# Projections by seven block products: queries, keys and values of a masked attention layer on one core

## The chip, the cores and the metric

One Trainium2 chip, one of its cores. The time is the device time of one launch in microseconds (us), the median of several runs. Engines of the core: TensorE (PE in the profile; PEld is its loading of stationary operands), VectorE (DVE), ScalarE (ACT), GpSimd (POOL) and SyncE (SP), which here only issues DMAs. Each engine runs its own queue of instructions in order; queues wait for each other by semaphores.

## The reference

32 graphs of 512 nodes with 512 features share one adjacency matrix. Layer 0 is a masked attention of 8 heads of 64 features, layer 1 a graph convolution; each is added to its input and normalised over the features. All is float32.

```
q, k, v = x @ Wq + bq, x @ Wk + bk, x @ Wv + bv      # each 512x512 by 512x512, per graph
scores = q k^T / 8 + (0 where adj else -1e9)         # per head
out = softmax(scores) @ v
x = layernorm(x + out)
y = adj @ x                                          # per graph
x = layernorm(x + y @ weight + bias)
```

## The kernel before

One fast path does the work (a general path follows only if a check at the end asks for it; here it does not run). Its order is written out by hand in program order; the tile framework adds only the waits. All matrices are held as four blocks of 128 rows, on 128 partitions.

**Projections.** `x_transpose(b, c)` (L264) turns one block of graph b's rows by TensorE and ScalarE copies it into `xT`. `project_qk(b, hp, which)` (L272) makes one block of 128 features of the queries or keys, transposed: four matmuls of 128x128 stationary and 512 moving columns into one bank of PSUM. ScalarE takes the bank for queries (L281), VectorE for keys (L283). `project_v` (L285) does the same for one block of rows of the values, taken by VectorE (L292). That makes 12 units per graph. PSUM banks for everything but scores and attention outputs come from a ring of three, `bank` (L205): the n-th user waits until the (n-3)-th has been read.

**Attention.** The main loop runs over pairs (graph b, pair of heads hp). In each step it issues `scores` for the next pair of heads in two halves (matmuls L379, exponential on ScalarE L382, mask product on VectorE L383, running sum on GpSimd L386 and L388), with `attend` (L396) for the present pair between them. Every second step also adds up the denominators (L407), inverts them (`invert`, L420 to L423) and adds the attention output of two pairs to the rows (`residual`, L429 to L434).

**Work in between.** The end of each step takes units from a list that is made new for each graph (at hp = 0). It holds, in order: the 12 projection units of graph b+1; among them `normalise` of graph b-1 (both layer norms due: ScalarE takes a root, L317, VectorE a reciprocal and eight blocks of rows, L321), `split` of graph b-1 (rows into a rounded part `high` and a rest `low`, one operation of 128x2048 each, L327 and L328) and `store` of graph b-2; then `aggregate` (adj @ x, eight matmuls on the high and low parts, L350, in fp32r) alternating with the transposes of graph b+2; then `convolve` (y @ weight, L360, the sum on VectorE L362, after GpSimd has added the bias row, L355). Each unit has a weight (1.0, 0.6, 0.15 or 0), and `work_until` spreads the weights evenly over the four steps:

```
begin = share * (hp - begun) + (0.25 if hp % 2 else 0.0)
end = share * (hp - begun + 1) + (0.0 if hp % 2 else 0.25)
while units and (units[0][1] == 0 or done < begin + (end - begin) * part - 0.3):
```

**Loads.** The rows of a graph are loaded once, into one of four buffers `xs`, which is transposed, added to, normalised and at last stored. All DMAs go through SP's queue, in program order. At the start the three projection weights are loaded whole, in rows of 2 KB.

Of the kernel before, what the change touches and what calls it, by code (L numbers as in the profile page):

```python
# [27 lines left out]
FP = mybir.dt.float32  # L31
# [8 lines left out]
NEG = -1.0e9  # L40
P = 128
HD = 64
GROUP = 4
BOUND = 1.0e20


def load_row(nc, pool, v, name):
    t = pool.tile([P, v.shape[0]], FP, name=name)
    nc.sync.dma_start(t, bass.AP(tensor=v.tensor, offset=v.offset, ap=[[0, P], [1, v.shape[0]]]))
    return t  # L50


def load_col(nc, pool, v, name):
    t = pool.tile([P, v.shape[0] // P], FP, name=name)
    nc.sync.dma_start(t, v.rearrange("(c p) -> p c", p=P))
    return t


def load_weight(pool, w, name, queue):
    t = pool.tile([P, w.shape[0] // P, w.shape[1]], FP, name=name)  # L60
    queue.dma_start(t, w.rearrange("(c p) f -> p c f", p=P))
    return t
# [127 lines left out]
def fast_kernel(ctx: ExitStack, tc, verdict, x, adj, Wq, bq, Wk, bk, Wv, bv, W1, b1, out):  # L190
# [14 lines left out]
    def bank(*shape):  # L205

        return psum.tile([P, *shape], FP, name="bank", tag="bank", bufs=3)


    X = {}  # L210

    def load(b, by_block=False):
        X[b] = work.tile([P, NB, D], FP, name="xs", bufs=4)
        if by_block:
            for c in range(NB):
                nc.sync.dma_start(X[b][:, c, :], x[b, c * P:(c + 1) * P, :])
        else:
            nc.sync.dma_start(X[b], x[b].rearrange("(c p) d -> p c d", p=P))

    load(0, by_block=True)  # L220
    wq = load_weight(consts, Wq, "wq", nc.sync)
    wk = load_weight(consts, Wk, "wk", nc.sync)
    bq_c = load_col(nc, consts, bq, "bq_c")
    bk_c = load_col(nc, consts, bk, "bk_c")
    adj_s = work.tile([P, NB, N], FP, name="yT", bufs=1)
    nc.sync.dma_start(adj_s, adj.rearrange("(c p) m -> p c m", p=P))
    wv = load_weight(consts, Wv, "wv", nc.sync)
    bv_r = load_row(nc, consts, bv, "bv_r")
    for b in range(1, min(3, B)):
        load(b)  # L230
    w1 = load_weight(consts, W1, "w1", nc.sync)
    b1_r = load_row(nc, consts, b1, "b1_r")

    ident = consts.tile([P, P], FP, name="ident")
    make_identity(nc, ident)
# [25 lines left out]

    XT, QT, KT, V = {}, {}, {}, {}

    def x_transpose(b, c):  # L264
        if c == 0:
            XT[b] = work.tile([P, DB, N], FP, name="xT", bufs=1)
        pt = bank(DB, P)
        for d in range(DB):
            nc.tensor.transpose(pt[:, d, :], X[b][:, c, d * P:(d + 1) * P], ident)
        nc.scalar.activation(XT[b][:, :, c * P:(c + 1) * P], pt, AF.Copy)  # L270

    def project_qk(b, hp, which):  # L272
        w, bias, store, name = (wq, bq_c, QT, "qT") if which == 0 else (wk, bk_c, KT, "kT")
        if hp == 0:
            store[b] = work.tile([P, HP, N], FP, name=name)
        pm = bank(N)
        for d in range(DB):
            nc.tensor.matmul(pm, w[:, d, hp * P:(hp + 1) * P], XT[b][:, d, :],  # L278
                             start=(d == 0), stop=(d == DB - 1))
        if which == 0:  # L280
            nc.scalar.activation(store[b][:, hp, :], pm, AF.Identity, bias=bias[:, hp:hp + 1])  # L281
        else:
            nc.vector.tensor_scalar(store[b][:, hp, :], pm, bias[:, hp:hp + 1], None, op0=ALU.add)  # L283

    def project_v(b, c):  # L285
        if c == 0:
            V[b] = work.tile([P, NB, D], FP, name="v")
        pm = bank(D)
        for d in range(DB):
            nc.tensor.matmul(pm, XT[b][:, d, c * P:(c + 1) * P], wv[:, d, :],  # L290
                             start=(d == 0), stop=(d == DB - 1))
        nc.vector.tensor_add(V[b][:, c, :], pm, bv_r)  # L292

    def flips(b):
        return [(x_transpose, b, c) for c in range(NB)] if b < B else []

    def projections(b):
        if b >= B:
            return []
        units = [(project_qk, b, hp, w) for hp in range(HP) for w in range(2)]  # L300
        return units + [(project_v, b, c) for c in range(NB)]

# [16 lines left out]
            nc.vector.tensor_scalar(row, row, STAT[t][:, slot, 0:1], rstd[:, slot:slot + 1],  # L321
                                    op0=ALU.subtract, op1=ALU.mult)

    def split(b):
        high = HIGH[b] = work.tile([P, NB, D], FR, name="high", bufs=1)
        low = LOW[b] = work.tile([P, NB, D], FR, name="low", bufs=1)
        nc.scalar.activation(high, X[b], AF.Copy)  # L327
        nc.vector.tensor_sub(low, X[b], high.bitcast(FP))  # L328

    def norms(t):  # L330

        parts = [(normalise, t, range(2 * NB if t > 0 else NB)), (split, t)]
        return parts + [(store, t - 1)] * (t > 0) if t >= 0 else []

    def store(b, blocks=None):
        for c in blocks or ():
            nc.sync.dma_start(out[b, c * P:(c + 1) * P, :], X[b][:, c, :])
        if blocks is None:
            nc.sync.dma_start(out[b].rearrange("(c p) d -> p c d", p=P), X[b])


    YT = {}

    def aggregate(b, d):
        if d == 0:
            YT[b] = work.tile([P, DB, N], FP, name="yT", bufs=1)
        pm = bank(N)
        for part in (LOW[b], HIGH[b]):
            for m in range(NB):
                nc.tensor.matmul(pm, part[:, m, d * P:(d + 1) * P], adjT[:, m, :],  # L350
                                 start=(part is LOW[b] and m == 0), stop=(part is HIGH[b] and m == NB - 1))
        nc.scalar.activation(YT[b][:, d, :], pm, AF.Copy)  # L352
        if d == DB - 1:
            for c in range(NB):
                nc.gpsimd.tensor_add(X[b][:, c, :], X[b][:, c, :], b1_r)  # L355
# [7 lines left out]
        statistics(b, 1, c)  # L363

    def aggregation(b):
        return [(aggregate, b, d) for d in range(DB)] if b >= 0 else []

    def convolution(b):
        return [(convolve, b, c) for c in range(NB)] if b >= 0 else []
# [4 lines left out]
    def scores(b, hp, half):  # L374
        for j in (2 * half, 2 * half + 1):
            ps = psum.tile([P, 2, N], FP, name="ps", bufs=2)
            for s in range(2):
                lanes = slice(s * HD, (s + 1) * HD)
                nc.tensor.matmul(ps[:, s, :], KT[b][lanes, hp, j * P:(j + 1) * P], QT[b][lanes, hp, :],  # L379
                                 start=True, stop=True)  # L380
            e = E[b, hp, j] = work.tile([P, 2, N], FP, name="e", bufs=6)
            nc.scalar.activation(e, ps, AF.Exp, scale=1.0 / root)  # L382
            nc.vector.tensor_mul(e, e, edge[:, j, None, :].to_broadcast([P, 2, N]))  # L383
            if j == 1:
                ES[b, hp] = work.tile([P, 2, N], FP, name="es", bufs=3)
                nc.gpsimd.tensor_add(ES[b, hp], E[b, hp, 0], e)  # L386
            elif j > 1:
                nc.gpsimd.tensor_add(ES[b, hp], ES[b, hp], e)  # L388

    def attend(b, hp):  # L390
        po = psum.tile([P, N], FP, name="po", bufs=1)
        for j in range(NB):
            e = E.pop((b, hp, j))
            for s in range(2):
                h = 2 * hp + s
                nc.tensor.matmul(po[s * HD:(s + 1) * HD, :], V[b][:, j, h * HD:(h + 1) * HD], e[:, s, :],  # L396
                                 start=(j == 0), stop=(j == NB - 1))
        AT[b, hp] = work.tile([P, N], FP, name="attT")
        nc.scalar.activation(AT[b, hp], po, AF.Copy)
# [55 lines left out]
    def run(units):  # L455
        for unit in units:
            unit[0](*unit[1:])

    first = projections(0)
    run(flips(0) + first[:4])  # L460
    for c in range(NB):
        adjacency(c)
        run(first[4 + 2 * c:6 + 2 * c])

    pairs = [(b, hp) for b in range(B) for hp in range(HP)]
    scores(*pairs[0], 0)
# [2 lines left out]
    for i, (b, hp) in enumerate(pairs):  # L469
        if hp == 0:  # L470


            units = [(u, 1.0) for u in projections(b + 1)]
            for k, chore in enumerate(norms(b - 1)):
                units.insert(2 * k + 1, (chore, 0.0))
            gather, turn = aggregation(b - 1), flips(b + 2)
            for k in range(NB):
                units += [(u, 0.6) for u in gather[k:k + 1]] + [(u, 0.15) for u in turn[k:k + 1]]
            if b < B - 1:
                units += [(u, 1.0) for u in convolution(b - 1)]  # L480

            begun = 0 if b < B - 1 else 1
            share = sum(w for _, w in units) / (HP - 2 * begun)
            done = 0.0
        if hp == 1 and b > 0 and b + 2 < B:
            load(b + 2)

        def work_until(part):

# [26 lines left out]
            run([u for u, _ in units])  # L516
    run([u for u, _ in units])
    t = B - 1
    rest = convolution(t - 1)
    run(rest[:2])  # L520
    invert(t, 1)
    residual(t, 2)
    residual(t, 3)
    normalise(t, range(NB))
    split(t)
    run(rest[2:])
    if t > 0:
        normalise(t, range(NB, 2 * NB))
        store(t - 1)
    run(aggregation(t))  # L530
    judge()
    for c in range(NB):
        convolve(t, c)
# [26 lines left out]
```

## Time and profile before

| | before |
|---|---|
| median of 3 runs | 3242.62 us (3241.83 to 3243.03) |
| the profiled execution | 3243.45 us, span 3241.7 us |
| its mean granted TensorE clock | 0.997 |
| VectorE, ScalarE, GpSimd busy | 1498.2, 995.7, 1183.0 us |
| matmuls of the projections, busy | wq 466.8, wk 463.5, wv 456.4 us |
| matmuls of scores, attention, convolution, busy | 510.7, 467.7, 458.2 us |
| rows of normalise (L321), mean of one | 646 ns |
| DMA moved | 74.73 MB, mean 23 GB/s |

The profile is of one execution. A line of its list of groups gives the source line, engine and operation, the output and inputs with partitions and elements, the number of instructions, the busy time in us and the mean duration of one in ns, then the engine's idle time just before them and what ended it. Matmuls are pipelined, so that the mean duration of one is longer than the distance from one to the next. A line of the timeline has a start and a duration in us, and merges neighbours of one kind; in brackets stand the idle time before it and what ended that.

### The profile page before, as it was taken

What the parts mean: (1) busy time and instruction counts of PE and PEld (TensorE: products, weight loads), DVE (VectorE), ACT (ScalarE), POOL (GpSimd) and SP (SyncE); (2) the same over time, 40 slices, a digit from 0 to 9 for tenths busy, and PEclk for the clock granted to TensorE, in tenths of its full rate; (3) what the DMA queues carried; (4) which work ended last, traced back from release to release, by engine and by line L of the source; (5) the groups of instructions that cost most, each with busy time, mean ns of one, the idle gap of its engine ahead of it and who ended that gap; (6) DMA issues with size and microseconds to landing.
All of it is one profiled execution on the core that took longest, in us unless ns stands there. A gap on an engine that the chain in (4) does not pass through costs nothing. (4 is left out here: it accounts for less than half of the span.)

```text
span 3241.7 us, 27725 instructions
## 1 busy us (share of the span) xinstructions
PE 3209.3 (99%) x11026; PEld 1421.8 (44%) x11026; DVE 1498.2 (46%) x2077; ACT 995.7 (31%) x1285; POOL 1183.0 (36%) x585
## 2 busy tenths in 40 slices
PE   9999999999999999999999999999999999999998
PEld 4444444444444444444444444444444444444444
DVE  4444544435444344444444444544435444345455
ACT  2323332232332323322323223232232332333322
POOL 2433343333334333343234333333333334333443
PEclk9999999999999999999999999999999999999999
DMA  3000000000000000000000000000000000000001
GB/s 123 1 1 26 26 26 14 13 26 26 27 26 1 26 26 27 26 1 26 27 26 26 9 18 26 26 27 22 5 26 26 26 26 1 26 26 26 14 1 40
DMA packets 38008, 74.73 MB, mean 23 GB/s; under 512 B 2288, under 2 KB 2288, under 8 KB 37872
## 3 DMA queue, kind: packets, MB, share of 16 engines
q1 hardware_dynamic: 37872, 72.89, 6.4%
q8 instruction: 89, 1.46, 0.2%
q14 instruction: 47, 0.39, 0.0%
HBM read 39.33 MB, written 33.55 MB: 22 GB/s over the span
## 5 line engine op out<-in xcount | busy, mean ns | idle before, releaser
L383 DVE TENSOR_TENSOR e<-e,edge 128x1024 f32<-128x1024 f32 x512 | 611.5, 1236 | 892.7 <-ACT e L382 892.7
L386 POOL TENSOR_TENSOR es<-e 128x1024 f32<-128x1024 f32 x128 | 302.1, 2360 | 1722.9 <-DVE e L383 1722.9
L388 POOL TENSOR_TENSOR es<-es,e 128x1024 f32<-128x1024 f32 x256 | 710.1, 2774 | 273.3 <-DVE e L383 263.2
L382 ACT ACTIVATE e<-ps 128x1024 f32<-128x1024 f32 x512 | 496.7, 1021 | 953.9 <-PE ps L379 953.5
L379 PE MATMUL ps<-qT,kT 64*128 64x512 f32 x2048 | 510.7, 617 | 5.0 <-ACT e L382 5.0
L278 PE MATMUL bank<-xT,wq 128*128 128x512 f32 x1024 | 466.8, 599 | 2.1 <-DMA wq<-in_L_gnn_Wq_dram 2.1
L396 PE MATMUL po<-e,v 128*64 128x512 f32 x2048 | 467.7, 598 | 0.0
L278 PE MATMUL bank<-xT,wk 128*128 128x512 f32 x1024 | 463.5, 595 | 0.0
L360 PE MATMUL bank<-w,yT 128*128 128x512 f32 x1024 | 458.2, 596 | 0.6 <-DVE inverse L422 0.4
L290 PE MATMUL bank<-wv,xT 128*128 128x512 f32 x1024 | 456.4, 598 | 0.0
L379 PEld LDWEIGHTS ps<-qT,kT 64*128 64x128 f32 x2048 | 176.5, 186 | 310.1 <-issue 248.8
L278 PEld LDWEIGHTS bank<-xT,wq 128*128 128x128 f32 x1024 | 192.7, 191 | 256.8 <-issue 249.7
L290 PEld LDWEIGHTS bank<-wv,xT 128*128 128x128 f32 x1024 | 189.3, 190 | 244.0 <-issue 237.8
L278 PEld LDWEIGHTS bank<-xT,wk 128*128 128x128 f32 x1024 | 189.7, 190 | 238.7 <-issue 238.7
L360 PEld LDWEIGHTS bank<-w,yT 128*128 128x128 f32 x1024 | 187.2, 190 | 206.1 <-issue 200.4
L396 PEld LDWEIGHTS po<-e,v 128*64 128x64 f32 x2048 | 135.6, 136 | 315.9 <-issue 314.1
L281 ACT ACTIVATE qT<-bank,bq_c 128x512 f32<-128x512 f32 x128 | 87.5, 683 | 470.6 <-PE bank L278 470.6
L292 DVE TENSOR_TENSOR v<-bank,bv_r 128x512 f32<-128x512 f32 x128 | 88.6, 692 | 244.4 <-PE bank L290 244.4
L352 ACT ACTIVATE yT<-bank 128x512 f32<-128x512 f32 x128 | 76.5, 597 | 348.8 <-PE bank L350 348.8
L283 DVE TENSOR_SCALAR kT<-bank,bk_c 128x512 f32<-128x512 f32 x128 | 95.8, 748 | 183.2 <-PE bank L278 183.2
L311 DVE BATCH_NORM_STATS2 bnst<-xs 128x6 f32<-128x512 f32 x256 | 174.6, 682 | 5.5
L362 DVE TENSOR_TENSOR xs<-bank,xs 128x512 f32<-128x512 f32 x128 | 85.5, 668 | 193.7 <-POOL xs L355 186.2
(55 smaller groups left out, 1931.3 us busy)
## 6 DMA issues: line engine op xcount, KB each, us to landing
xs<-in_x_dram SPq DMA_DIRECT2D x31, 1024.0 KB, 5.2
out_dram<-xs SPq DMA_DIRECT2D x31, 1024.0 KB, 4.2
xs<-in_x_dram SPq DMA_DIRECT2D x4, 256.0 KB, 3.9
wq<-in_L_gnn_Wq_dram SPq DMA_DIRECT2D x1, 1024.0 KB, 8.0
wk<-in_L_gnn_Wk_dram SPq DMA_DIRECT2D x1, 1024.0 KB, 10.6
yT<-in_adj_dram SPq DMA_DIRECT2D x1, 1024.0 KB, 10.2
wv<-in_L_gnn_Wv_dram SPq DMA_DIRECT2D x1, 1024.0 KB, 11.2
w<-in_L_gnn_weight_dram SPq DMA_DIRECT2D x1, 1024.0 KB, 14.0
```

The costliest lines, as they stand in the source:

```text
L278: nc.tensor.matmul(pm, w[:, d, hp * P:(hp + 1) * P], XT[b][:, d, :], start=(d == 0), stop=(d == DB - 1))
L283: nc.vector.tensor_scalar(store[b][:, hp, :], pm, bias[:, hp:hp + 1], None, op0=ALU.add)
L290: nc.tensor.matmul(pm, XT[b][:, d, c * P:(c + 1) * P], wv[:, d, :], start=(d == 0), stop=(d == DB - 1))
L292: nc.vector.tensor_add(V[b][:, c, :], pm, bv_r)
L311: nc.vector.bn_stats(st, X[b][:, c, :])
L360: nc.tensor.matmul(pm, YT[b][:, d, c * P:(c + 1) * P], w1[:, d, :], start=(d == 0), stop=(d == DB - 1))
L379: nc.tensor.matmul(ps[:, s, :], KT[b][lanes, hp, j * P:(j + 1) * P], QT[b][lanes, hp, :], start=True, stop=True)
L382: nc.scalar.activation(e, ps, AF.Exp, scale=1.0 / root)
L383: nc.vector.tensor_mul(e, e, edge[:, j, None, :].to_broadcast([P, 2, N]))
L386: nc.gpsimd.tensor_add(ES[b, hp], E[b, hp, 0], e)
L388: nc.gpsimd.tensor_add(ES[b, hp], ES[b, hp], e)
L396: nc.tensor.matmul(po[s * HD:(s + 1) * HD, :], V[b][:, j, h * HD:(h + 1) * HD], e[:, s, :], start=(j == 0), stop=(j == NB - 1))
```

## The change

Every 512x512 projection is cut into two by two blocks of 256 and computed by seven block products in place of eight (Strassen's scheme in Winograd's form). The sums of blocks of the weights are made once (`combine`, on VectorE); those of the transposed rows are made for each graph (in `x_transpose`: s1 by VectorE straight from PSUM, three more by GpSimd). A product is four matmuls of 256 moving columns, in one bank. Products 1 and 5 are put down as they come (by ScalarE for queries and keys, VectorE for values), the others are added to what lies there by VectorE, and after product 7 GpSimd adds blocks to one another twice. A projection's products run in the order 1, 5, 6, 7, 2, 3, 4; in the list, products 1 and 5 of the next projection stand ahead of 3 and 4 of the one before. So there are 21 units of weight 0.5 per graph.

The queries, keys and values of a graph become two tiles each, of three buffers in all. The transposes read a copy of the rows of their own, `xin`, loaded by blocks; the rows that are worked on, `xs`, have two buffers, and `turn_over` stores graph b-2 and loads graph b into its place. `split` and the aggregation go by blocks of 128 features, the first two splits between the last three products. The weights are loaded in two halves of columns.

```
+FACTORS = {1: ("A11", "B11"), 2: ("A12", "B21"), 3: ("S4", "B22"), 4: ("A22", "T4"),
+           5: ("S1", "T1"), 6: ("S2", "T2"), 7: ("S3", "T3")}
+ORDER = (1, 5, 6, 7, 2, 3, 4)
...
+    def load(b):
+        X[b] = work.tile([P, NB, D], FP, name="xs")
+        nc.sync.dma_start(X[b], x[b].rearrange("(c p) d -> p c d", p=P))
+
+    def load_blocks(b):
+
+        for c in range(NB):
+            IN[b, c] = work.tile([P, D], FP, name="xin", bufs=NB)
+            nc.sync.dma_start(IN[b, c], x[b, c * P:(c + 1) * P, :])
+
+    def load_factors(w, name):
+        t = consts.tile([P, 7, 2, half], FP, name=name)
+        for s in range(2):
+            nc.sync.dma_start(t[:, 2 * s:2 * s + 2, :, :].rearrange("p a c f -> p (a c) f"),
+                              w[:, s * half:(s + 1) * half].rearrange("(c p) f -> p c f", p=P))
+        return t
...
+    def combine(w, bias):
+
+        b11, b21, b12, b22, t1, t2, t4 = (w[:, i, :, :] for i in range(7))
+        nc.vector.tensor_sub(t1, b12, b11)
+        nc.vector.tensor_sub(b12, b22, b12)
+        nc.vector.tensor_sub(t2, b22, t1)
+        nc.vector.tensor_sub(t4, b21, t2)
+        width = bias.shape[1] // 2
+        nc.vector.tensor_sub(bias[:, width:], bias[:, width:], bias[:, :width])
...
         for d in range(DB):
-            nc.tensor.transpose(pt[:, d, :], X[b][:, c, d * P:(d + 1) * P], ident)
-        nc.scalar.activation(XT[b][:, :, c * P:(c + 1) * P], pt, AF.Copy)
...
+            nc.tensor.transpose(pt[:, d // 2, d % 2, :], IN[b, c][:, d * P:(d + 1) * P], ident)
+        below, cols = c // 2, slice(c % 2 * P, (c % 2 + 1) * P)
+        nc.scalar.activation(xt[:, 2 * below:2 * below + 2, :, cols], pt, AF.Copy)
+        a11, a12, a21, _, s1, s2, s4 = (xt[:, i, :, :] for i in range(7))
+        if below:
+            nc.vector.tensor_add(s1[:, :, cols], pt[:, 1, :, :], a21[:, :, cols])
+        if c == NB - 1:
+            nc.gpsimd.tensor_sub(s2, s1, a11)
+            nc.gpsimd.tensor_sub(a21, a11, a21)
+            nc.gpsimd.tensor_sub(s4, a12, s2)
+
+    def project(b, which, i):
...
+        if i == 1:
+            store[b] = [work.tile([P, NB, half] if values else [P, 2, N], FP, name=which, bufs=3) for _ in range(2)]
...
+        pm = bank(2, half)
+        for r in range(2):
+            for d in range(2):
+                nc.tensor.matmul(pm[:, r, :], left[:, d, r * P:(r + 1) * P], right[:, d, :],
+                                 start=(d == 0), stop=(d == 1))
+        add = nc.vector.tensor_add
+        if i in (1, 5):
+            out_, s = (c11, 0) if i == 1 else (c22, 1)
+            if values:
+                add(out_, pm, bias[:, None, s * half:(s + 1) * half].to_broadcast([P, 2, half]))
+            else:
+                for r in range(2):
+                    nc.scalar.activation(out_[:, r, :], pm[:, r, :], AF.Identity,
+                                         bias=bias[:, 2 * s + r:2 * s + r + 1])
+        elif i == 6:
+            add(c12, pm, c11)
+        elif i == 7:
+            add(c21, pm, c12)
+            nc.gpsimd.tensor_add(c12, c12, c22)
+            nc.gpsimd.tensor_add(c22, c22, c21)
+        else:
+            into = {2: c11, 3: c12, 4: c21}[i]
+            add(into, pm, into)
...
+        units = [(project, b, which, i) for which in "qkv" for i in ORDER]
+        for n in (5, 12):
+            units[n:n + 4] = units[n + 2:n + 4] + units[n:n + 2]
+        return units
...
+    def split(b, d):
+        high = HIGH[b, d] = work.tile([P, NB, P], FR, name="high")
+        low = LOW[b, d] = work.tile([P, NB, P], FR, name="low")
+        cols = X[b][:, :, d * P:(d + 1) * P]
+        nc.scalar.activation(high, cols, AF.Copy)
+        nc.vector.tensor_sub(low, cols, high.bitcast(FP))
...
+    def turn_over(b):
+        store(b - 2)
+        load(b)
...
-    run(flips(0) + first[:4])
+    run(first[:5])
+    combine(wk, bk_c)
+    run(first[5:9])
     for c in range(NB):
         adjacency(c)
-        run(first[4 + 2 * c:6 + 2 * c])
+        run(first[9 + c:10 + c])
+    combine(wv, bv_r)
+    run(first[13:])
...
+            units = [(u, 0.5) for u in projections(b + 1)]
+            if b > 0:
+                units.insert(2, ((normalise, b - 1, range(2 * NB if b > 1 else NB)), 0.0))
+            if b > 1:
+                units.insert(6, ((turn_over, b), 0.0))
             gather, turn = aggregation(b - 1), flips(b + 2)
...
+            if turn and gather:
+                units[-2:-2], gather = [(gather[0], 0.0)], gather[1:]
+                units[-1:-1], gather = [(gather[0], 0.0)], gather[1:]
+            for unit in gather:
+                units.append((unit, 0.55 if unit[0] is aggregate else 0.0))
+                if unit[0] is aggregate:
+                    units += [(u, 0.13) for u in turn[:1]]
+                    turn = turn[1:]
+            units += [(u, 0.13) for u in turn]
             if b < B - 1:
                 units += [(u, 1.0) for u in convolution(b - 1)]
...
-    split(t)
+    run(gather[:2])
     run(rest[2:])
+    run(gather[2:])
     if t > 0:
         normalise(t, range(NB, 2 * NB))
         store(t - 1)
-    run(aggregation(t))
     judge()
```

## The prediction

> **What bounds the kernel now.** I read the page first (shares, slices, groups), then one steady batch in the timeline, then stretches of it line by line.
>
> ```profile
> PE 3209.3 (99%) x11026; PEld 1421.8 (44%) x11026; DVE 1498.2 (46%) x2077; ACT 995.7 (31%) x1285; POOL 1183.0 (36%) x585
> L278 PE MATMUL bank<-xT,wq 128*128 128x512 f32 x1024 | 466.8, 599 | 2.1 <-DMA wq<-in_L_gnn_Wq_dram 2.1
> ```
>
> TensorE never waits: its instructions in order set the end; the other engines are under half full. The x1024 is 32 batches x 4 units x 4 matmuls x 2: each float32 matmul is two records, "halves" below. The timeline of a steady batch (start, duration, engine, line, what):
>
> ```profile
> 1050.44 3.70 PE L278 MATMUL bank<-xT,wq 128*128 128x512 f32 x8
> 1052.19 5.62 POOL L388 TENSOR_TENSOR es<-es,e 128x1024 f32<-128x1024 f32 x2 [1.56 <-DVE e L383]
> 1053.98 3.60 PE L278 MATMUL bank<-xT,wk 128*128 128x512 f32 x8
> 1054.18 0.69 ACT L281 ACTIVATE qT<-bank,bq_c 128x512 f32<-128x512 f32 x1 [2.48 <-PE bank L278]
> 1054.89 1.28 ACT L317 ACT_TABLE_LOAD   x1
> 1056.18 0.30 ACT L317 ACTIVATE rstd<-stat,eps 128x8 f32<-128x8 f32 x1
> 1056.75 4.53 DVE L321 TENSOR_SCALAR xs<-xs,stat,rstd 128x512 f32<-128x512 f32 x8
> 1057.41 3.60 PE L278 MATMUL bank<-xT,wq 128*128 128x512 f32 x8
> 1060.85 3.60 PE L278 MATMUL bank<-xT,wk 128*128 128x512 f32 x8
> 1061.21 0.74 DVE L283 TENSOR_SCALAR kT<-bank,bk_c 128x512 f32<-128x512 f32 x1
> ...
> 1087.07 1.04 PE L429 MATMUL bank<-ident,attT 128*128 128x128 f32 x8
> ```
>
> Units follow at 3.435 us (1057.41 to 1060.85): 429.3 ns a half. The 1053.98 unit ends at 1057.4, but VectorE takes its bank only at 1061.21, behind the eight rows of normalise. That delay costs nothing now: the three-bank ring gives a bank back two units (6.9 us) after its own. The batch repeats after 100.0 us (the same scores start at 1016.54 and 1116.54). So a change in TensorE's work counts in full, and so does every new wait for a bank.
>
> **The products.** Removed per batch: 12 units x 3.435 = 41.2 us. Added: 21 products, each 4 matmuls of 256 columns, so 8 halves. No row shows a half of 256 columns. Below: half of 429.3, 214.7 ns. Above: the fp32r matmul of aggregate has the same weights to load and, in one record of 512 columns, about as long a stream:
>
> ```profile
> 3110.70 1.09 PE L350 MATMUL bank<-adjT,high 128*128 128x512 f32 x4
> 3111.63 1.10 PE L350 MATMUL bank<-adjT,low 128*128 128x512 f32 x4
> 3112.56 1.10 PE L350 MATMUL bank<-adjT,high 128*128 128x512 f32 x4
> 3113.50 1.10 PE L350 MATMUL bank<-adjT,low 128*128 128x512 f32 x4
> ```
>
> Four in 0.933 us, 233 ns each. Transposes (float32, 128 columns, a 128x128 load each) follow at (1.04 - 0.276)/7 = 109 ns. From 128 to 512 columns that is (429.3 - 109)/3 = 106.8 for 128 columns and 2.3 fixed, though a load comes with each; so 256 columns give 216 ns. I take 216, as these rows are float32, and fp32r, with one record for 512 columns where float32 has two, streams in another way. A product is 1.73 us (bounds 1.72 and 1.865), 21 are 36.3: **-4.9 us a batch** (-5.1 to -2.1).
>
> **Evictions.** VectorE loses 8 (k, v) and gains 17 adds of 0.69 (row of L362: 128x512 from PSUM) and two of half the width for s1; GpSimd gains 9 operations of 1.24 (L355: four in 4.95); ScalarE has two 256-column evictions for products 1 and 5 of q and k, 0.47 each (0.683 less 256 x 0.83 ns, the slope between its 512 and 1024 rows). VectorE goes from 46 to about 53 of 100 us, GpSimd from 37 to 48: neither becomes the bound. But units are half as long, so the ring covers only 3.5 us. I walk the list against the timeline, with t=0 at 1050.44 and its like, where the units of a pair of heads begin. Which units fall to which pair follows from the weights: 21 x 0.5 + 4 x 0.55 + 4 x 0.13 + 4 = 17.2, a quarter for each, and 0.25 more for an even pair.
>
> *First pair of heads (9 products).* The order is q1 q5 normalise q6 q7 q2 store/load k1 k5 q3 q4. ScalarE evicts q1 and q5 (3.8 to 4.75), loads its table and takes the root to 6.35; VectorE's reciprocal and eight rows run to 11.05 (now: 10.77). Only then comes q6's add, to 11.8. TensorE has done q2 at 8.85, and k1 needs q6's bank: it starts at 12.05, its first weight load exposed. **+3.2 us** (2.4 to 4). Queued behind normalise are the adds of q6, q7, q2; GpSimd's two for q7 come at 12.5, early enough for q3's add. Normalise is delayed no further than now.
>
> *Second pair (8).* k6 k7 k2, invert, v1 v5, two residuals, k3 k4 v6: every bank comes back before its turn (closest: k3, needing v5's add at 10.4, starts at 10.5). 0 (up to +0.7, one late add).
>
> *Third pair.* v7 v2 split v3 split v4 aggregate flip aggregate. v3's add needs GpSimd's c12+c22, which follows v7's add (3.45) but stands behind the two es additions, which run to 7.36 (1052.19 + 5.62 less 1050.44). So v3's add waits to 8.65 and ends at 9.4, v4's at 10.7, each holding the split behind it. TensorE is at 9.0 after the first aggregate; the first flip needs v3's bank (+0.67 with its load), the next aggregate v4's (+0.86). **+1.5** (0 to 2.2).
>
> *Last pair.* The bias rows on GpSimd come a pair of heads earlier; the 0.4 us that TensorE now loses around invert, behind conv's add, goes: **-0.4**. The three GpSimd subtractions after the last flip (3.7 us) have 20 us of cover before q6; without it they would delay q6.
>
> **Queues and loads.** SP issues four more 256 KB loads a batch, behind the store and the 1 MB load that now share a moment. Normalise done at 11.05, store 4.2, load 5.2 (the landing times of the profile): the rows are there at 21, and the residual needs them at 38; the blocks have longer. Cost 0; without the cover VectorE's residual adds would wait. Splitting by feature blocks changes no TensorE work.
>
> **Sum**, against the profiled span of 3241.7. Batches 2 to 29: -4.9 + 3.2 + 1.5 - 0.4 = -0.6, x28 = -17. Batch 0 (no normalise, a wait of 0.9 allowed): -4. Batch 1 (four rows, so 2.3 us less of the first wait): -3. Batch 30 has no flips between its products, so the first split waits for v4's add: 4.4 in place of 1.5, +2. Start: fewer products (-4.9), but VectorE has twelve subtractions of 0.69, nine adds more and four adjacency groups of 2.75 us on it, which now hold the banks: +8 by the same walk, so +3 (-2 to +8; rows of 1 KB in the weight loads included). End: the split before the last aggregation (1.91 + 2.29 us, with TensorE idle 5.94) becomes blocks of about 1.25, and less clock is lost: -4 (-8 to +3, if the late load of the last batch holds its residual). Together -23: span 3219, and with the 1.8 us around it (run 3243.45, span 3241.7) **3220 us**. The run lies 0.8 above the median of 3242.62, which changes nothing.
>
> **The clock.** The trace shows what a long gap does:
>
> ```profile
> 3162.34 3.78 PE L379 MATMUL ps<-qT,kT 64*128 64x512 f32 x8 [4.43 <-ACT e L382]
> ```
>
> and by stretches (busy time of each engine, then the granted clock):
>
> ```profile
> 3160.00:3164.00 4.00, 1.67 (x4) 0.84 (x6) 3.96 (x3) 3.99 (x5) 0.00 (x0) 0.55 0.69 262
> 3168.00:3172.00 4.00, 4.00 (x25) 3.06 (x24) 3.83 (x7) 0.60 (x1) 3.59 (x2) 1.00 0.00 0
> ```
>
> After 4.43 us of idleness the granted clock is 0.55 and eight halves take 3.78 instead of 1.99; with the next four that is 2.3 us lost. No steady gap in the trace is over 0.5 us, so 3.2 lies between; by 0.5 nothing is lost, by 4.43 2.3 us. I take 0, and the other as a rival. The Trainium skill (TensorE: Matmul & The Clock Gate, Why this matters for your kernels) speaks against the change here: it asks for no gaps over about 3 us between bursts, or the clock halves. By that page an estimate is 1.7 us (half of the 3.4 us window of its Part 1) for each of 29 gaps, and the sum would be 3269.
>
> **Rivals.**
> *Short streams cost 233 ns* (the fp32r row; against it, the transposes): +2.8 us a batch, of which the waits swallow 1.2, since they end when VectorE does: +1.6 x 29, and twice 2.8 for batch 0 and the start: 3272, slower. It decides from about 220 ns. Chance 0.25.
> *The waits are smaller.* If GpSimd is not behind, the third pair's 1.5 goes: 3220 - 44 = 3176. If normalise cost nothing too, 3220 - 44 - 29 x 3.2 = 3083. For it: VectorE is half idle; against: its queue is strictly in order in every line read. Chance 0.15, a third of it the last.
> *The gap of 3.2 us halves the clock* in each batch: 28 x 2.3 = 64, so 3284, slower. It decides between 0.5 and 4.4 us of idleness. Chance 0.12.
> Mixtures: 0.06.
>
> **How the numbers follow.** My forecast, 0.42, has its own range of 3195 to 3245 (the two waits off by 0.8 us together). Within 0.2%, what a measurement here can't tell from no change, is 3236 to 3249. Faster: 0.34 of the forecast, 0.15 and 0.02 of mixtures, 0.51. Same: 0.06, 0.02 from the short-stream case at its low end, 0.01: 0.09. Slower: 0.02 + 0.23 + 0.12 + 0.03 = 0.40. The range 3165 to 3290 leaves out the waitless end and the worst mixtures.
>
> **What would show it.** Eight halves of a product should start 1.73 us apart from the next product's. In each steady batch TensorE should be idle once for about 3 us, released by VectorE's add of q6 behind L321's rows, and twice for under 1 us around the first flip; its busy share should fall to some 95%, with the granted clock at 1.00 throughout. Wrong if products follow at 1.86, if the clock dips once a batch, or if no such idle time is there.

## The result, and the profile after

The changed kernel takes 3419.29 us (median of 4 runs, 3418.24 to 3422.08) against 3242.41: 1.0547 of the time before, interval 1.0529 to 1.0565. It is slower, far outside the range; the forecast was 3220. The page of the changed kernel, shares first, then two groups of product matmuls (x1792 is 32 batches x 7 products x 8 halves):

```profile
PE 3202.6 (94%) x13330; PEld 1950.6 (57%) x13330; DVE 1860.1 (54%) x2540; ACT 1029.9 (30%) x1509; POOL 1572.0 (46%) x873
...
L338 PE MATMUL bank<-xT,wk 128*128 128x256 f32 x1792 | 499.6, 442 | 121.4 <-DVE q L350 118.8
...
L338 PE MATMUL bank<-xT,wq 128*128 128x256 f32 x1792 | 402.8, 382 | 1.1 <-DMA wq<-in_L_gnn_Wq_dram 1.1
```

The same 1792 halves cost 402.8 us for q and 499.6 for k, with a mean duration of 382 and 442 ns: something slows k's products alone. And ahead of them stand 118.8 us of waiting for VectorE, 30 times 4.0 us. The timeline of the first pair of heads of one steady batch shows both (units begin at 2045.35):

```profile
2045.35 8.90 PE L338 MATMUL bank<-xT,wq 128*128 128x256 f32 x40
2045.72 3.94 DVE L458 TENSOR_TENSOR e<-e,edge 128x1024 f32<-128x1024 f32 x2 [0.78 <-ACT e L457]
...
2048.67 5.92 POOL L463 TENSOR_TENSOR es<-es,e 128x1024 f32<-128x1024 f32 x2 [1.23 <-DVE e L458]
...
2049.96 1.28 ACT L386 ACT_TABLE_LOAD   x1
2051.26 0.30 ACT L386 ACTIVATE rstd<-stat,eps 128x8 f32<-128x8 f32 x1
...
2051.83 5.78 DVE L390 TENSOR_SCALAR xs<-xs,stat,rstd 128x512 f32<-128x512 f32 x8
2057.53 0.68 DVE L350 TENSOR_TENSOR q<-bank,q 128x512 f32<-128x512 f32 x1
...
2058.27 6.69 PE L338 MATMUL bank<-xT,wk 128*128 128x256 f32 x16 [4.02 <-DVE q L350]
...
2064.80 3.62 PE L338 MATMUL bank<-xT,wq 128*128 128x256 f32 x16
```

TensorE finishes five products of q, and VectorE is in normalise. The add of q6 comes at 2057.53, and only then does k1 start. Then 16 halves take 6.5 us (2058.27 to 2064.80), where the next 16 take 3.46. By stretches (busy times of the engines, then the granted clock):

```profile
2054.00:2058.00 4.00, 0.25 (x2) 0.00 (x0) 4.00 (x8) 0.00 (x0) 0.59 (x1) 0.94 0.00 0
2058.00:2061.00 3.00, 2.73 (x7) 2.20 (x8) 1.50 (x3) 0.00 (x0) 1.77 (x2) 0.50 0.81 309
2061.00:2064.50 3.50, 3.50 (x10) 2.82 (x9) 0.00 (x0) 0.84 (x2) 0.77 (x1) 0.53 0.40 115
2064.50:2067.50 3.00, 3.00 (x16) 2.64 (x15) 0.69 (x1) 0.84 (x2) 0.00 (x0) 1.00 1.02 370
```

The clock is 0.50 behind the wait (in the trace's record of the granted clock, from 2057.49 to 2064.32) and 1.00 after it. The same happens on a smaller scale in the third pair of heads:

```profile
2001.54 1.29 POOL L353 TENSOR_TENSOR v<-v 128x512 f32<-128x512 f32 x1
...
2002.87 0.69 DVE L357 TENSOR_TENSOR v<-bank,v 128x512 f32<-128x512 f32 x1 [3.51 <-POOL v L353]
...
2003.62 0.66 PE L307 MATMUL bank<-ident,xin 128*128 128x128 f32 x4 [0.71 <-DVE v L357]
...
2005.39 1.33 PE L419 MATMUL bank<-adjT,low 128*128 128x512 f32 x4 [1.11 <-DVE v L357]
...
2006.51 1.91 PE L419 MATMUL bank<-adjT,high 128*128 128x512 f32 x4
2008.22 1.05 PE L307 MATMUL bank<-ident,xin 128*128 128x128 f32 x4
...
2008.93 1.53 PE L419 MATMUL bank<-adjT,low 128*128 128x512 f32 x4
```

Two waits, 0.71 and 1.11 us, with one group of transposes between them; then four high parts take 1.91 in place of 1.09 and the transposes 1.05 in place of 0.60. The record has the clock at 0.50 here from 2006.29 to 2009.71.

A batch, measured from one square-root table load of ScalarE to the next (2049.96, 2155.77), takes 105.81 us, and 100.00 before. The parts per steady batch, the measured ones from such batch times of the runs below:

| part | forecast | measured | from |
|---|---|---|---|
| products, and the end of conv's wait | -4.9 - 0.4 | -5.3 | e9: 94.67 less 100.00 |
| wait of k1 for q6's bank | +3.2 | +4.2 | after less e1 with a slow third pair: 105.81 - 98.53 = 7.3, less the next row |
| slower clock behind it | 0 | +3.1 | 6.53 us for 16 halves, 3.46 at full clock |
| waits in the third pair | +1.5 | +2.3 | e1 with no slow stretch less e9: 96.98 - 94.67 |
| slower clock behind them | 0 | +1.5 | e1 with and without: 98.53 - 96.98 |
| sum | -0.6 | +5.8 | 105.81 - 100.00 |

### The profile page after: what moved, and what is told of

The parts are those of the page before. It is cut to its first block, busy times and chain, and to the rows that moved or that the text cites. A ratio compares the mean times of both kernels' runs of the same rounds, so it can differ in the third digit from the quotient of the medians.

```text
span 3417.4 us, 33960 instructions
## 1 busy us (share of the span) xinstructions
PE 3202.6 (94%) x13330; PEld 1950.6 (57%) x13330; DVE 1860.1 (54%) x2540; ACT 1029.9 (30%) x1509; POOL 1572.0 (46%) x873
## 5 line engine op out<-in xcount | busy, mean ns | idle before, releaser
L338 PE MATMUL bank<-xT,wk 128*128 128x256 f32 x1792 | 499.6, 442 | 121.4 <-DVE q L350 118.8
L338 PEld LDWEIGHTS bank<-xT,wk 128*128 128x128 f32 x1792 | 394.1, 225 | 229.0 <-DVE q L350 130.9
L455 PE MATMUL ps<-q,k 64*128 64x512 f32 x2048 | 511.6, 618 | 4.3 <-ACT e L457 4.3
L338 PE MATMUL bank<-wv,xT 128*128 128x256 f32 x1792 | 407.8, 382 | 5.9 <-DVE v L357 2.6
L338 PE MATMUL bank<-xT,wq 128*128 128x256 f32 x1792 | 402.8, 382 | 1.1 <-DMA wq<-in_L_gnn_Wq_dram 1.1
L338 PEld LDWEIGHTS bank<-wv,xT 128*128 128x128 f32 x1792 | 335.8, 190 | 73.6 <-issue 26.4
L455 PEld LDWEIGHTS ps<-q,k 64*128 64x128 f32 x2048 | 176.9, 187 | 288.7 <-issue 229.0
L423 POOL TENSOR_TENSOR xs<-xs,b_r 128x512 f32<-128x512 f32 x128 | 159.8, 1281 | 228.6 <-DVE low L398 228.6
L419 PE MATMUL bank<-adjT,low 128*128 128x512 f32 x512 | 169.3, 455 | 42.4 <-DVE v L357 32.3
L390 DVE TENSOR_SCALAR xs<-xs,stat,rstd 128x512 f32<-128x512 f32 x256 | 186.5, 796 | 1.4
```

The costliest lines, as they stand in the source:

```text
L338: nc.tensor.matmul(pm[:, r, :], left[:, d, r * P:(r + 1) * P], right[:, d, :], start=(d == 0), stop=(d == 1))
L419: nc.tensor.matmul(pm, part, adjT[:, n % NB, :], start=(n == 0), stop=(n == 2 * NB - 1))
L455: nc.tensor.matmul(ps[:, s, :], keys[:, j * P:(j + 1) * P], queries, start=True, stop=True)
```

## The experiments

The theory: per batch two waits for one of the three banks, and a lower clock behind each, make the loss; the products themselves are as cheap as forecast. Rivals: VectorE has become the bound, so that any order waits somewhere; or the denser work of short halves lowers the clock, not idleness. Ratios are to the kernel before, run beside each.

| run | us | ratio (interval) |
|---|---|---|
| e1_norm_later | 3188.81 | 0.9839 (0.9823 to 0.9856) |
| e2_v_pairs_dve | 3369.21 | 1.0391 (1.0373 to 1.0408) |
| e3_fill_matmuls | 3324.72 | 1.0251 (1.0234 to 1.0269) |
| e3t_fill_transposes | 3325.98 | 1.0257 (1.0240 to 1.0274) |
| e8_fill_two | 3324.48 | 1.0259 (1.0242 to 1.0276) |
| e7_no_es | 3180.59 | 0.9814 (0.9798 to 0.9830) |
| e10_more_work | 3422.26 | 1.0560 (1.0544 to 1.0576) |
| e5_reordered | 3130.74 | 0.9662 (0.9646 to 0.9678) |
| e6_reordered_judge | 3127.17 | 0.9650 (0.9634 to 0.9666) |
| e9_splits_ahead | 3084.32 | 0.9520 (0.9507 to 0.9533) |

**Normalise three units later (e1_norm_later).**

```
-                units.insert(2, ((normalise, b - 1, range(2 * NB if b > 1 else NB)), 0.0))
+                units.insert(5, ((normalise, b - 1, range(2 * NB if b > 1 else NB)), 0.0))
```

> One edit to the changed kernel: normalise is put behind q2 in the list instead of between q5 and q6, so that the adds of q6, q7 and q2 are ahead of it on VectorE. The whole output is computed. Theory (two waits per batch for a PSUM bank, and a lower TensorE clock behind each): the 4.0 us wait of k1 for q6's bank goes (with its exposed load 4.4), and so does the slow stretch behind it, where 16 halves took 6.5 us instead of 3.46. 29 batches x 7.4 = 215, so about 3204 us. Rival A (VectorE is too full; the wait only moves to q3, q4 or the next scores): well over 3300. Rival B (the clock falls because halves of 256 columns with a weight load each are denser work, not because of idleness): only 4.4 x 29 = 128 goes, 3291, and the mean granted clock stays near 0.95.

One number moved, and 230 us went: 3188.81, 1.6% faster than the kernel before. The timeline of the same place:

```profile
2016.65 3.62 PE L338 MATMUL bank<-xT,wk 128*128 128x256 f32 x16
2016.83 1.27 POOL L353 TENSOR_TENSOR q<-q 128x512 f32<-128x512 f32 x1
2016.85 0.69 DVE L357 TENSOR_TENSOR q<-bank,q 128x512 f32<-128x512 f32 x1 [1.03 <-PE bank L338]
...
2017.69 4.84 DVE L390 TENSOR_SCALAR xs<-xs,stat,rstd 128x512 f32<-128x512 f32 x8
```

k's products start with no wait ahead and at full speed, and normalise runs beside k1 and k5, whose banks go to ScalarE, and q3, whose add is the next that TensorE needs. So VectorE, busy for 58% of this run, is no bound, and the products are not what slows the clock: both rivals fall. It is 15 us better than expected: in 11 of 28 steady batches the clock did not fall in the third pair either (batches of 97.0 and of 98.5 us).

**The value sums on VectorE (e2_v_pairs_dve).**

```
-            nc.gpsimd.tensor_add(c12, c12, c22)
-            nc.gpsimd.tensor_add(c22, c22, c21)
+            pairs_on = nc.vector if values else nc.gpsimd
+            pairs_on.tensor_add(c12, c12, c22)
+            pairs_on.tensor_add(c22, c22, c21)
```

> One edit to the changed kernel: for the values, the two block sums after product 7 run on VectorE instead of GpSimd. The whole output is computed. Theory: the waits of the first transposes and the second aggregate (0.71 and 1.11 us, 2.0 with their loads) and the slow stretch behind them (8 matmuls and 4 transposes in 3.8 us instead of 2.3) go: 29 x 3.45 = 100, so about 3319 us. Rival A (VectorE is too full, its two more sums of 0.7 to 1.3 us make the wait anew): 3380 to 3440. Rival B (clock falls by dense work): 29 x 2.0 = 58, 3361.

Only half came, 50 us. The timeline of the third pair shows why:

```profile
2073.37 2.12 DVE L354 TENSOR_TENSOR v<-v 128x512 f32<-128x512 f32 x1
2075.53 2.72 DVE L355 TENSOR_TENSOR v<-v 128x512 f32<-128x512 f32 x1
...
2079.59 1.17 PE L420 MATMUL bank<-adjT,low 128*128 128x512 f32 x4 [2.42 <-DVE low L399]
```

Each sum took over 2 us, while GpSimd's running sums were in SBUF; the same two sums took 0.69 us each for the first graph (at 51.34 and 52.06), where GpSimd stood still. The splits behind them came late, and TensorE waited 2.42 us once a batch, with the clock at 0.50 behind it in 10 of 27 steady batches. The old waits were what they were taken for (both are gone); the edit made another. Rival A was half right here: not VectorE's share, but its order.

**Filling the wait (e3_fill_matmuls, e3t_fill_transposes, e8_fill_two).** Unread work behind q2, into the free bank of the attention output; with 32 transposes in place of the matmuls, or with two matmuls:

```
+    def filler():
+        idle = psum.tile([P, N], FP, name="po", bufs=1)
+        for n in range(4):
+            nc.tensor.matmul(idle, w1[:, n, 0:P], w1[:, n, :], start=True, stop=True)
...
+                units.insert(6, ((filler,), 0.0))
```

> The changed kernel with four matmuls of 128x512 put in behind q2, whose result nobody reads: they fill some 3.4 of the 4.4 us that TensorE waits before k1. The output is complete. Theory (idleness lowers the clock): the wait itself stays, filled, but k1 and k5 run at full clock, 3.46 us instead of 6.5: 29 x 3.1 = 90, about 3329 us, and the granted clock shows no dip there. Rival B (dense work lowers the clock): the dip stays or grows, 3419 or more.

> The same with 32 transposes of 128x128 (some 3.5 us) instead of the four matmuls. If transposes keep the clock up as matmuls do: 3329 us as well. If they don't, the dip stays: 3419 or a little more. I lean to the second, since in the changed kernel the clock also falls behind two waits of only 0.71 and 1.11 us that have 0.66 us of transposes between them.

> The changed kernel with two unread matmuls of 128x512 behind q2 instead of four (run e3_fill_matmuls): they leave about 2.6 us of idleness before k1. The output is complete. If the clock falls only after some 3.4 us without work, as the wait of 4.4 us had it: no dip there, 3325 us as with four. If a shorter idleness is enough when it falls in a certain place: dips in part of the batches, 3330 to 3419.

All three take 3325 us, 94 less than the changed kernel with more work in them. A batch takes 102.8 us for 105.81, and 101.3 in some (8 of 28 with four matmuls), where the third pair keeps its clock too. Of the run with two matmuls, the wait, then two such waits by stretches of 3.41 us (the first of them is the wait of this line; why these edges is told under e10_more_work):

```profile
2001.46 3.72 PE L338 MATMUL bank<-xT,wk 128*128 128x256 f32 x16 [2.30 <-DVE q L350]
...
1996.71:2000.12 3.41, 2.45 (x8) 1.07 (x6) 3.41 (x6) 0.00 (x0) 1.07 (x1) 1.00 0.00 0
2000.12:2003.53 3.41, 2.06 (x10) 1.83 (x11) 2.58 (x5) 0.03 (x1) 1.18 (x1) 1.00 0.50 196
...
972.71:976.12 3.41, 1.35 (x4) 0.28 (x2) 3.41 (x8) 0.00 (x0) 0.00 (x0) 1.00 0.00 0
976.12:979.53 3.41, 3.17 (x8) 2.55 (x9) 1.48 (x3) 0.00 (x0) 2.20 (x2) 0.50 0.81 308
979.53:982.95 3.42, 3.42 (x17) 3.03 (x16) 0.00 (x0) 1.68 (x4) 0.33 (x1) 1.00 0.52 123
```

k1 and k5 run at full clock behind 2.30 us of idleness, here and in all but 2 of 27 steady batches. So it is idleness that lowers the clock: 29 x 3.1 = 90 us of the loss. In the second wait shown the clock did fall: 2.06 of the 2.30 us lay in one stretch, where the first wait left 0.96 and 1.35 in two. Transposes keep the clock up as matmuls do; the lean of that expectation was wrong.

**No running sums (e7_no_es).**

```
-                nc.gpsimd.tensor_add(ES[b, hp], E[b, hp, 0], e)
...
-                nc.gpsimd.tensor_add(ES[b, hp], ES[b, hp], e)
+            ES[b, hp] = flat
```

> The changed kernel without GpSimd's running sums of the exponentials (384 operations of 2.4 to 2.8 us); the denominators come from a constant tile, so this part of the computation is left out. It tells why the wait behind normalise was 4.0 us and not 3.2: theory, VectorE's operations on SBUF run slower while GpSimd's run. Then normalise's eight rows take 4.5 us in place of 5.8 and the two mask products at the start of that stretch 2.4 in place of 3.9, and the wait shrinks to 2.5 to 3.1 us. The waits in the third pair go too, as GpSimd is free: 2.0 + 1.5. If the shorter wait still lowers the clock: 105.8 - 3.5 - 1.3 = 101.0 a batch, about 3280 us; if not, 98 a batch, about 3190. Rival (those rows take their time for another reason): L390's rows stay at 5.8 us, about 3320.

```profile
2013.09 3.75 DVE L392 TENSOR_SCALAR xs<-xs,stat,rstd 128x512 f32<-128x512 f32 x8
...
2017.49 5.41 PE L340 MATMUL bank<-xT,wk 128*128 128x256 f32 x16 [1.98 <-DVE q L352]
```

The eight rows take 3.75 us instead of 5.78, the wait 1.98 instead of 4.02: GpSimd's sums had doubled it. The clock still falls: k's 16 halves take 5.4 us here, and 21 of 28 steady batches take 98.6 us, the others 96.9. So 1.98 us can be enough, where 2.30 above mostly was not.

**More work in the changed kernel (e10_more_work).**

```
+                units += [((filler,), 0.0)] * (b > 1) + [(u, 1.0) for u in convolution(b - 1)]
```

> The changed kernel with one unread matmul of 128x512 more in each of batches 2 to 30, ahead of the first convolve, where TensorE never waits: 0.86 us more work a batch. The output is complete. In the changed kernel every steady batch took 105.81 us, to a few hundredths. If the clock returns at the edges of a window that runs on by itself, a slow stretch that starts later ends at the same edge, a batch locks to a whole number of windows (the Trainium skill, TensorE: Matmul & The Clock Gate, Part 1, gives 3.413 us, and 31 of them are 105.81), and the added work costs less than itself, down to nothing: 3419 to 3432. If the slow stretch has a length of its own: 3419 + 29 x 0.86 = 3444.

29 x 0.86 = 25 us of work cost 3 us. Batches now take 106.24 and 105.37 us in turn, 211.61 a pair. The window of 3.413 us that the Trainium skill gives (TensorE: Matmul & The Clock Gate, Part 1) goes into that 62.0 times, and 31.0 times into the 105.81 of the changed kernel. The traces agree. In the profiled execution of each kernel and run here, the edges of the granted clock all lie on one grid of 3.413 us, to 0.006 us, and every slow stretch of a steady batch is one step of that grid or two. TensorE's idle time in each step, from the matmul records, says when the clock falls. Over the steady batches of all these traces (300 to 2980 us), the clock fell behind each of the 80 steps at full clock in which TensorE was idle for more than 2.0 us, behind 152 of the 178 with 1.72 to 2.0 us, and behind none with less. A slow step was followed by another where 0.73 us or more of it was idle, and not at 0.48 or less. So the wait of 4.0 us, with 3.25 us in one step and 0.77 in the next, costs two slow steps, and the pair of shorter waits, 1.82 us in one step, costs one. A wait that comes later leaves less work in the slow steps behind it, so that added work can vanish; that this is what holds the batch at 31 steps is our reading.

**The way to a faster version (e5_reordered, e6_reordered_judge, e9_splits_ahead).** On top of e1, the third pair's list in another order, so that GpSimd has two aggregates' time for the value sums; then the check behind the second of the last convolve units; then the third and fourth split ahead of v3 and v4 (the comments name the runs):

```
...
-                units[-2:-2], gather = [(gather[0], 0.0)], gather[1:]
-                units[-1:-1], gather = [(gather[0], 0.0)], gather[1:]
...
+                s0, s1, g0, s2, g1, s3, g2, g3 = gather
+                last = units[-2:]
+                units[-4:] = ([(s0, 0.0), (s1, 0.0)] + units[-4:-2] + [(g0, 0.55), (g1, 0.55)]
+                              + last + [(s2, 0.0), (s3, 0.0)])          # e5, e6
+                units[-4:] = ([(s0, 0.0), (s1, 0.0)] + units[-4:-2]
+                              + [(g0, 0.55), (s2, 0.0), (g1, 0.55), (s3, 0.0)] + last)   # e9
...
+        if c == 1:
+            judge()                                                     # e6, e9
```

> The kernel with normalise behind q2 (run e1_norm_later), and with the third pair's list in another order: split split v7 v2 aggregate aggregate v3 v4 split split, then transposes and aggregates in turn, so that GpSimd has two aggregates' time more for v's block sums. The whole output is computed. Theory (the two remaining waits, 0.72 and 1.11 us with some 0.2 us of exposed load each, and the 1.55 us of low clock behind them in 20 of 29 batches): a batch of 94.9 us in place of 96.98 or 98.5, so 3188.8 - 29 x 2.1 - 20 x 1.55 = 3097 us, granted clock near 0.995. If VectorE's order makes a new wait instead: 3150 to 3190.

> The same with the check's small operations (judge) issued behind the second of the last four convolve units, where the changed kernel issues them ahead of the first: there TensorE waits 5.0 us for VectorE, which still has the last normalise of the graph before. The whole output is computed. Theory: 4 to 5 us less than e5_reordered, and no slow clock behind that wait: 3088 to 3093. If the end is bound by VectorE anyway: no difference.

> The kernel of run e6_reordered_judge with the third and fourth split ahead of v3 and v4: split split v7 v2 aggregate split aggregate split v3 v4, then transposes and aggregates. The whole output is computed. In e5 and e6 the third aggregate waited 1.09 us in every batch for a split queued on VectorE behind v4's add. Theory: that wait goes, with its load 1.15 us, so a batch takes 94.85 us in place of 96.00: 3127 - 29 x 1.15 = 3094 us, clock 0.997. If the splits then hold v3's and v4's banks and the wait only changes place: 3115 to 3130.

e5 missed by 34 us, 3130.74: the old waits went, and the edit made a new one in every batch of 96.00 us, the third aggregate behind a split that stood in VectorE's queue after v4's add:

```profile
2029.22 0.69 DVE L357 TENSOR_TENSOR v<-bank,v 128x512 f32<-128x512 f32 x1 [1.02 <-PE bank L338]
...
2029.83 1.28 DVE L398 TENSOR_TENSOR low<-xs,high 128x512 fp32r<-128x512 f32 x2
2030.66 1.17 PE L419 MATMUL bank<-adjT,low 128*128 128x512 f32 x4 [1.09 <-DVE low L398]
```

Behind these 1.09 us the clock never fell. e6 lies 3.6 us lower at overlapping spreads; its profile has 2.6 us of waiting at the check for 5.1. e9 takes that last wait away: a batch of 94.67 us, 3084.32 us in all, 4.8% faster than the kernel before. Its page:

```profile
PE 3042.5 (99%) x13330; PEld 1858.0 (60%) x13330; DVE 1821.7 (59%) x2540; ACT 1026.9 (33%) x1509; POOL 1579.2 (51%) x873
```

TensorE is the bound again, with the saving of the products in full: 5.3 us a batch.

## Why the prediction was wrong

**The clock: the step that failed.** "I take 0, and the other as a rival": the fall of the clock behind the waits had its own rival, at 0.12, priced at 2.3 us for a batch. It cost 3.1 + 1.5 = 4.6, so about 29 x 4.6 = 133 of the 199 us between forecast and result. Two things were wrong in it. The trace of before showed 0 at 0.5 us and 2.3 at 4.43, and a wait of 3.2 is nearer to the second; the text took the first. And the third pair's waits were not looked at for it at all. The rule that stood beside it, about 3 us without work (the Trainium skill, TensorE: Matmul & The Clock Gate, Why this matters for your kernels), pointed the right way. The runs differ from it in size: the clock fell behind 1.98 us in e7 and behind 0.71 + 1.11 us in the changed kernel, and mostly did not behind 2.30 in e8. What decides is how much idle time lies in one step of the 3.413 us grid: over 2.0 us always lowered the clock, under 1.72 never. By these figures, as an estimate, a wait of 3.2 us keeps the clock only if an edge falls into its middle 0.8 us, in about a quarter of the positions.

**The first wait: right mechanism, undersized.** It is where and why the forecast put it (q6's add behind normalise, the bank owed to k1), but 4.2 us and not 3.2: 29 us over 29 batches. The walk took normalise's 4.53 us from a batch of the kernel before, where only its first rows met GpSimd's sums. VectorE's mask products ahead of the next pair's units, in the kernel before and in the changed one:

```profile
1045.81 2.33 DVE L383 TENSOR_TENSOR e<-e,edge 128x1024 f32<-128x1024 f32 x2
1050.82 2.36 DVE L383 TENSOR_TENSOR e<-e,edge 128x1024 f32<-128x1024 f32 x2 [2.68 <-ACT e L382]
...
2042.62 2.33 DVE L458 TENSOR_TENSOR e<-e,edge 128x1024 f32<-128x1024 f32 x2
```

They ended 2.3 us before the units began (at 1050.44), and now end 0.4 us before (at 2045.35); why they come later was not taken apart. GpSimd's sums start later with them, so that the next mask products and normalise now run while GpSimd does: 3.94 for 2.36 and 5.78 for 4.53. e7 shows that this is the cause. The Trainium skill has the rule (SBUF — State Buffer, SBUF: two separate sides): a GpSimd instruction and certain VectorE ones lock one pair of ports, and the later one waits for the whole of the other. The median row of normalise here takes 0.535 us and the longest 2.722, about one running sum of 2.85. In the batch shown the second row begins at 2052.29, behind the start of a running sum (2051.95), and ends at 2054.87, behind that sum's end (2054.59). The rule agrees, and a walk that moves VectorE's work against GpSimd's has to use it.

**The waits of the third pair: right**, 2.3 for 1.5, in both places and for the reason given (GpSimd's block sums behind its running sums; e7, without running sums, has neither wait); 23 us in 29 batches.

**The products: right.** Halves of 256 columns follow at 216 ns, so the rival of short streams (233 ns) is out. e9 shows the saving whole.

**Start and end**: +3 and -4 were forecast. TensorE reaches the first scores at 56.0 us, 0.8 earlier than before, so the start was overpriced by some 4 us. The end is dearer than forecast: from batch 30's square root to the end, the changed kernel takes 17 us more than the one before; the first wait of batch 30 with its slow clock, counted above, is 7 of them. Batch 30's first split holds TensorE for 4.2 us, and the check, which now comes behind the last normalise, for 5.0. The rest of the end was not taken apart.

**The rivals.** That the waits are smaller is out by their measured sizes. The likeliest case and the clock rival share their mechanism; the second was the true one, and its 3284 was too low because it left out the slow clock in the third pair, and sized the waits and the first slow stretch too small.

## What to carry to other kernels

When TensorE's units get shorter, a ring of banks covers less time: walk each in-order queue against it, and put long work on VectorE behind the evictions that TensorE needs next; one index in a list was worth 230 us here. Price a new gap of TensorE at its length and the slow clock behind it, also where it is under 3 us: in these runs what counted was the idle time within one step of 3.413 us, and from about 1.7 to 2.0 us on it cost at least one step at half clock. And where VectorE's and GpSimd's work on SBUF slide into each other, take their durations from a place where they overlap.

## What was not expected of the hardware

- A wait of 0.71 and one of 1.11 us with transposes between them lowered the clock for 3.41 us in each of the 27 batches of 105.8 us of the changed kernel, and in 17 of 28 of e1's with the same two waits.
- The granted clock moved on a fixed grid of 3.413 us and went by the idle time in the step before: 2.30 us of idleness, mostly split by an edge, lowered it in 2 of 27 steady batches, and 1.98 us in 21 of 28.
- In the changed kernel batches locked to 105.81 us, 31.0 windows of 3.413 us, and 25 us of added work cost 3.
- An add of VectorE from SBUF to SBUF took 2.12 and 2.72 us while GpSimd was adding, and 0.69 while it was not.
